# A two-layer graph network on one core: fp32 products in the first layer's sums, shorter lags at the layers' ends, and part of a normalisation on VectorE

## The chip, the core and the metric

The kernel runs on one core of a Trainium2 chip. The metric is the device time of one execution in microseconds, taken as the median of several runs. Beside it there is one profiled execution, whose trace gives the start and the length of every instruction on every engine. The engines are PE (TensorE, the matrix multiplier; its weight loads are listed as PEld), DVE (VectorE), ACT (ScalarE), POOL (GpSimd) and SP (SyncE, which here only issues DMAs). Each works through its own queue in order, and they meet through semaphores. DMAs are issued from the SP, ACT and POOL queues.

## The reference

There are 12,500 nodes with 64 features and 212,500 edges, sorted by their target `dst`. Each edge has a source `src`, a type from 0 to 15 and 8 attributes. Two layers run one after the other, and the second reads all of what the first has made:

```python
h = jnp.maximum(_layernorm(x, axis=-1), 0.0)
x = x + L0(h, weight, src, dst, edge_type)        # 16 matrices of 64 x 64
h = jnp.maximum(_layernorm(x, axis=-1), 0.0)
x = x + L1(h, src, dst, edge_attr, W1, b1, W2, b2)

# L0: sum over edges of  h[src] @ weight[type]           into dst
# L1: sum over edges of  relu([h[src], h[dst], attr] @ W1 + b1) @ W2 + b2   into dst
```

Everything is fp32.

## The kernel before

**Tiles and groups.** The edges are cut into 1,664 tiles of 128 (1,661 with edges in them), four tiles make a group (`G = 4`), and there are 416 groups (`NGR`). The nodes stand in 98 blocks of 128 (`NB`). Because the edges are sorted by target, the targets of one tile lie in a window of 12 nodes (`WT`) and those of one group in a window of 40 (`W`). A check in front finds out whether that holds; if it does, the kernel goes through `in_order()` (L272), which is what the profile shows, and otherwise through another path that the change leaves as it is.

**Front.** `x` is loaded in nine chunks of 6, 14, 14, 14, 14, 14, 12, 6 and 4 blocks (`FRONT`). For each chunk, `rows_of_sources` (L205) takes mean and variance on VectorE, the root on ScalarE, and then one ScalarE instruction per block makes `h` (L211). The SP queue writes each chunk of `h` to `h_rows` in HBM (L212).

**Gather.** `gather` (L397) issues one indirect DMA per tile from POOL (L402): 128 rows of 64 fp32 numbers, named by a column of `src_i`, into a tile `rows` that is buffered 14 deep. Both layers use it, the first with `h_rows`, the second with `a_rows`.

**First layer** (`first_layer`, L550). A loop over turns, `it`, handles several groups in one turn, each at another stage. In turn `it`, POOL gathers group `it` and ScalarE makes its one-hots, `oh_r`, over 16 relations times 12 nodes (`relations`, L410). One turn later (`L1_HI`) ScalarE rounds the gathered rows to bf16, two turns later (`L1_LO`) VectorE makes two more bf16 parts from what is left (three instructions), three turns later (`L1_PE`) PE multiplies the three parts by the bf16 one-hots, in two halves of 96 columns each, so 24 matmuls per group; and six turns later (`L1_ADD`) VectorE adds each tile's product into a table of relations by nodes (`table`), at a place that is read into a register. When the last group that touches two blocks has been added (the groups in `FIN`, at the end 408, 412 and 415), `finish` (L471) begins for these blocks: it multiplies the table by the 16 matrices (`pT`, fp32), adds to `x`, normalises, transposes, multiplies by the first two parts of `W1` and writes `a_rows` (fp32) and `b_rows` (bf16 parts) from the SP queue. `finish` is a generator; the loop takes one to three of its steps after each addition. Other generators cut in the same way are `attributes`, which splits the edge attributes into three bf16 parts, and `codes`, which makes the next piece of the one-hots' codes.

**Order.** `InOrder` (L443, whose line L452 stands for nearly all instructions of both layers in the profile) ties each engine's instructions to the order in which the program issues them. An instruction that waits therefore holds up all that was written behind it on its engine. POOL's gathers are not tied to the other engines except by their data: a gather needs a free `rows` buffer, and the first gather of a layer needs the whole of the table that it reads from, so the first layer's waits for the last write of `h_rows` and the second's for the last write of `a_rows`.

**Second layer** (`second_layer`, L653). The same kind of loop. In turn `it` POOL gathers rows of `a_rows`, SP loads `bw` and `at`, ScalarE makes one-hots and PE forms `pz`; three turns later VectorE adds the rows (`z`), four turns later ScalarE applies the relu (`hid`), six turns later PE sums over the edges by fp32 one-hots (`pa`), nine turns later VectorE adds into `sums`. `results` (L632) multiplies finished blocks by `W2`, adds `x` and writes the output from the ACT queue.

Of the kernel before, what the change touches and what calls it, by code (L numbers as in the profile page):

```python
# [37 lines left out]
ALU = mybir.AluOpType  # L39
# [37 lines left out]
L1_HI, L1_LO, L1_PE, L1_ADD = 1, 2, 3, 6  # L77
L2_Z, L2_HID, L2_PE, L2_ADD = 3, 4, 6, 9
# [38 lines left out]
def gnn_kernel(  # L117
# [69 lines left out]
    with ExitStack() as c1:  # L187
# [17 lines left out]
        def rows_of_sources(b0, nb):  # L205
            mv, rs = stats(wk, b0, nb, "r")
            off = wk.tile([P, nb], F32, name="r_off")
            V.scalar_tensor_tensor(off, mv[:, :, 0], -1.0, rs, op0=ALU.mult, op1=ALU.mult)
            h = wk.tile([P, nb, D], F32, name="r_h", bufs=4)
            for k in range(nb):  # L210
                S.activation(h[:, k, :], x3[:, b0 + k, :], AF.Relu, bias=off[:, k : k + 1], scale=rs[:, k : k + 1])  # L211
            nc.sync.dma_start(h_rows[b0 * P : (b0 + nb) * P, :].rearrange("(b p) c -> p b c", p=P), h)  # L212
# [59 lines left out]
    def in_order():  # L272
        with ExitStack() as c2:
# [36 lines left out]
            NHID = L2_PE - L2_HID + 3  # L310
# [99 lines left out]
            def relations(code, k, n):  # L410

                off = wk.tile([P, G, RW], BF16, name="off_r")
                oh = wk.tile([P, G, RW], BF16, name="oh_r", bufs=L1_PE + 2)
                for i in range(n):
                    S_.activation(off[:, i, :], iota_s, AF.Abs, bias=code[:, k + i : k + i + 1])
                S_.activation(oh[:, :n, :], off[:, :n, :], AF.Relu, bias=1.0, scale=-1.0)
                return oh

            def windows(row, k, top, engine):
                with behind(engine.engine):  # L420
                    _, vals = nc.values_load_multi_w_load_instructions(
                        row[0:1, k : k + RG],
                        engines=(engine.engine.engine,),
                        min_val=0,
                        max_val=top,
                        skip_runtime_bounds_check_because="targets are nodes, within the step's table by the check in front",
                    )
                return vals
# [33 lines left out]
            def go_on(k):  # L462

                n = BLOCKS[k][1] * P
                S_.copy(tables[(k + 1) % 2][:, :, :AHEAD], tables[k % 2][:, :, n : n + AHEAD])
# [84 lines left out]
            def first_layer(psA):  # L550
# [5 lines left out]
                n_of, oh_of, rows_of, parts_of, pa_of = {}, {}, {}, {}, {}  # L556
                chunk = 0
                for it in range(NGR + L1_ADD):
# [15 lines left out]
                    g = it - L1_HI  # L574
                    n = n_of.get(g, 0)
                    if n:
                        parts_of[g] = wk.tile([P, G, 3, D], BF16, name="parts", bufs=L1_PE + 2)
                        S_.copy(parts_of[g][:, :n, 0, :], rows_of[g][:, :n, :])
                    g = it - L1_LO
                    n = n_of.get(g, 0)  # L580
                    if n:
                        parts, left = parts_of[g], rows_of.pop(g)[:, :n, :]
                        lo = wk.tile([P, G, D], F32, name="left")[:, :n, :]
                        V_.tensor_tensor(lo, left, parts[:, :n, 0, :], op=ALU.subtract)
                        V_.tensor_copy(parts[:, :n, 1, :], lo)
                        V_.tensor_tensor(parts[:, :n, 2, :], lo, parts[:, :n, 1, :], op=ALU.subtract)
                    g = it - L1_PE
                    a = it - L1_ADD
                    if n_of.get(g, 0):

                        pa_of[g] = psA.tile([P, G, HW], F32, name="pa", bufs=5)
                    for i in range(G):
                        if i < n_of.get(g, 0):
                            for j in range(3):
                                for half in range(2):
                                    T_.matmul(
                                        pa_of[g][half * D : (half + 1) * D, i, :],
                                        lhsT=parts_of[g][:, i, j, :],
                                        rhs=oh_of[g][:, i, half * HW : (half + 1) * HW],
                                        start=(j == 0),  # L600
                                        stop=(j == 2),
                                    )
                        if a < 0:
                            continue
                        k = a * G + i
                        if i < n_of[a]:
                            ca, ka = divmod(k, NT // NCH)
                            if k % RG == 0:
                                at = windows(codes_of[ca][1], ka, SN + AHEAD - WT, V_)
                            to = tables[STEP[a] % 2][:, :, bass.ds(at[k % RG], WT)]  # L610
                            V_.tensor_tensor(
                                to, to, pa_of[a][:, i, :].rearrange("p (r n) -> p r n", r=RH), op=ALU.add
                            )
                        for _ in range(1 if a <= FIN[NREG - 1] else 2 if a <= FIN[NFIN - 2] else 3):
                            next(open_step, None)
                        next(coming, None)
                        if i % 2:
                            next(beside, None)
                    if a in FIN:
                        k = FIN.index(a)  # L620
                        for _ in open_step:
                            pass
                        if k + 1 < NFIN:
                            go_on(k)
                        open_step = finish(k, psA)
# [27 lines left out]
            def second_layer(ps):  # L653
# [6 lines left out]
                for it in range(NGR + L2_ADD):  # L660
# [39 lines left out]
                    g = it - L2_Z  # L700
                    n = n_of.get(g, 0)
                    if n:
                        z = wk.tile([P, G, D], F32, name="z", bufs=L2_HID - L2_Z + 2)
                        V_.tensor_tensor(z[:, :n, :], pz_of.pop(g)[:, :n, :], a_of.pop(g)[:, :n, :], op=ALU.add)
                        hid_of[g] = z
                    g = it - L2_HID
                    n = n_of.get(g, 0)
                    if n:
                        z = hid_of[g]
                        hid_of[g] = hid[g % NHID]  # L710
                        S_.activation(hid_of[g][:, :n, :D], z[:, :n, :], AF.Relu)
                        oh_of[g] = wk.tile([P, G, W], F32, name="oh", bufs=L2_PE - L2_HID + 2)
                        V_.tensor_tensor(
                            oh_of[g][:, :n, :],
                            bc(local[:, g * G : g * G + n], 2, W, [P, n, W]),
                            bc(iota_p, 1, n, [P, n, W]),
                            op=ALU.is_equal,
                        )
                    g = it - L2_PE
                    n = n_of.get(g, 0)  # L720
                    if n:
                        if g % 4 == 0:
                            pa = ps.tile([DA, 4, W], F32, name="pa", bufs=2)
                        pa_of[g] = pa[:, g % 4, :]
                        r, o = hid_of.pop(g), oh_of.pop(g)
                        for i in range(n):
                            T_.matmul(pa_of[g], lhsT=r[:, i, :], rhs=o[:, i, :], start=(i == 0), stop=(i == n - 1))
                    next(open_step, None)
                    g = it - L2_ADD
                    if g < 0:  # L730
                        continue
                    if n_of[g]:
                        if g % RG == 0:
                            at.update(enumerate(windows(place_row, g, SN + AHEAD2 - W, V_), g))
                        to = sums[STEP[g] % 2][:, bass.ds(at.pop(g), W)]
                        V_.tensor_tensor(to, to, pa_of.pop(g), op=ALU.add)
                    if g in FIN:
                        k = FIN.index(g)
                        for _ in open_step:
                            pass  # L740
                        if k + 1 < NFIN:
                            n = BLOCKS[k][1] * P
                            V_.tensor_copy(sums[(k + 1) % 2][:, :AHEAD2], sums[k % 2][:, n : n + AHEAD2])
                        open_step = results(k, ps)
# [459 lines left out]
```

## Time and profile before

| | |
|---|---|
| median of 3 runs | 4277.16 us (4273.73 to 4277.83) |
| profiled execution, its own time | 4275.86 us |
| its span, first to last instruction | 4274.1 us |
| busy: POOL | 3179.0 us (74%), 3,342 instructions |
| busy: ACT | 2041.7 us (48%), 4,300 instructions |
| busy: PE / weight loads | 1769.3 us (41%) / 1449.1 us (34%) |
| busy: DVE | 1421.0 us (33%), 5,311 instructions |
| HBM traffic | 56 GB/s over the span |
| granted TensorE clock | 1.00 of full speed |

A group row of the profile gives line, engine, operation, tiles and count, then busy time in all and mean ns of one, then the idle time of that engine just before these instructions and what ended it. A row of the timeline gives start and length in us, engine, line, operation, tiles, and in brackets the idle time before it and what ended that. A short line such as `DVE parts L452` in a wait names the engine, the tile and the line of what was waited for, by the profile's reckoning. A program's fp32 matmul stands in the trace as two records.

### The profile page before, as it was taken

Reading aid. Unit: us, or ns where it says so; the run is one execution under the profiler, and the core shown is the slowest. Engines: PE = TensorE matmul, PEld = TensorE weight load, DVE = VectorE, ACT = ScalarE, POOL = GpSimd, SP = SyncE. Lnnn points to the kernel's source line nnn. Section 1 sums busy time; section 2 is a strip of 40 time slices with the busy share of each in tenths; the row PEclk is TensorE's granted clock in tenths of the full one; section 3 lists DMA queues with packets and bytes.
Section 4 is the critical chain, followed back from the end, with each engine's and each line's share of the span. In section 5 each row is a group of like instructions: output and inputs, shape, how many; then the busy total and the mean of one; then the engine's idle time right before and its main releaser. Section 6 shows DMA issues by size and latency. Waiting matters only on the chain.

```text
span 4274.1 us, 61048 instructions
## 1 busy us (share of the span) xinstructions
PE 1769.3 (41%) x18622; PEld 1449.1 (34%) x18622; DVE 1421.0 (33%) x5311; ACT 2041.7 (48%) x4300; POOL 3179.0 (74%) x3342
## 2 busy tenths in 40 slices
PE   1454545555554545454543333333333333333333
PEld 1343434343343434343432222232322222232222
DVE  5444545445454454444421111111111111111111
ACT  6566666666666666565633333333333333333332
POOL 4777777777777777777757777777777777777776
DMA  5121212122222121111123333333333333333332
GB/s 128 38 43 40 47 39 47 40 44 42 44 42 43 40 42 35 30 31 30 31 67 72 71 70 73 70 69 74 70 69 74 70 69 74 69 70 74 70 72 41
DMA packets 289907, 241.93 MB, mean 57 GB/s; under 512 B 177128, under 2 KB 220144, under 8 KB 289464
## 3 DMA queue, kind: packets, MB, share of 16 engines
q0 software_dynamic: 106816, 110.79, 14.7%
q1 hardware_dynamic: 167241, 123.53, 10.7%
q10 hardware_dynamic: 15510, 3.61, 0.4%
q8 instruction: 149, 2.44, 0.2%
q14 instruction: 191, 1.56, 0.1%
HBM read 212.57 MB, written 25.10 MB: 56 GB/s over the span
## 4 chain that ended last, share of the span: by engine, by line
POOL 36%; DMA 34%; issue 19%; DVE 4%; ACT 4%; PE 1%; DVEq 0%; POOLq 0%; SPq 0%; ACTq 0%
POOL rows L402 36%; DMA rows<-h_rows,src_i 19%; DMA rows<-a_rows,src_i 14%; DVE parts L452 1%; DVE table L452 1%; DVE left L452 1%; DMA first_row<-in_first 1%; ACT parts L452 1%; ACT table L452 1%; ACT off_r L452 1%; PE pT L452 1%; PE pa L452 0%; ACT bp L452 0%; ACT attr_p L452 0%; POOLq L402 0%
## 5 line engine op out<-in xcount | busy, mean ns | idle before, releaser
L402 POOL DMA_INDIRECT rows<-h_rows,src_i x1661 | 1605.3, 966 | 545.6 <-issue 379.4
L402 POOL DMA_INDIRECT rows<-a_rows,src_i x1661 | 1567.2, 944 | 534.3 <-issue 461.8
L452 PE MATMUL pa<-oh_r,parts 128*64 128x96 bf16 x9966 | 649.3, 282 | 741.1 <-ACT parts L452 426.1
L452 ACT ACTIVATE hid<-z 128x256 f32<-128x256 f32 x416 | 173.1, 416 | 1343.4 <-DVE z L452 1309.4
L452 PE MATMUL pz<-bw,ohT 120*128 120x64 bf16 x1661 | 230.7, 240 | 1290.3 <-ACT ohT L452 1280.2
L452 PEld LDWEIGHTS <-parts 128*64 128x64 bf16 x9966 | 443.2, 158 | 927.4 <-ACT parts L452 465.7
L452 DVE TENSOR_TENSOR z<-pz,rows 128x256 f32<-128x256 f32 x416 | 176.5, 424 | 1712.7 <-DMA rows<-a_rows,src_i 1556.5
L452 PEld LDWEIGHTS <-ohT 120*128 120x128 bf16 x1661 | 165.0, 124 | 1351.5 <-ACT ohT L452 1345.1
L452 ACT ACTIVATE off_r<-iota_s,code 128x192 bf16<-128x192 f32 x1661 | 617.6, 443 | 1.7 <-DMA w1c<-w1c_p 1.7
L452 ACT CAST parts<-rows 128x256 bf16<-128x256 f32 x416 | 167.6, 403 | 736.3 <-DMA rows<-h_rows,src_i 735.8
L452 PE MATMUL pT<-wrel,table 128*128 128x64 f32 x1568 | 434.0, 434 | 113.8 <-DVE table L452 113.8
L452 DVE TENSOR_TENSOR table<-table,pa 128x96 f32 x1661 | 419.9, 253 | 123.4 <-issue 51.4
L452 PE MATMUL pa<-oh,hid 128*65 128x40 f32 x3322 | 448.4, 309 | 10.2 <-DVE sums L452 8.1
L452 PEld LDWEIGHTS pT<-wrel,table 128*128 128x128 f32 x1568 | 363.0, 323 | 161.5 <-DVE table L452 117.7
L452 PEld LDWEIGHTS pa<-oh,hid 128*65 128x65 f32 x3322 | 408.2, 230 | 10.5 <-issue 8.3
L452 DVE TENSOR_TENSOR left<-rows,parts 128x256 f32<-128x256 f32 x416 | 176.5, 424 | 565.3 <-ACT parts L452 564.1
L452 ACT ACTIVATE oh_r<-off_r 128x768 bf16<-128x768 bf16 x416 | 349.9, 841 | 13.0
L452 ACT ACTIVATE off<-local_bc,neg_w 120x512 bf16<-120x512 bf16 x416 | 294.2, 707 | 32.0 <-DVE sums L452 17.3
L452 ACT ACTIVATE ohT<-off 120x512 bf16<-120x512 bf16 x416 | 261.6, 629 | 13.0
L452 PE MATMUL pz<-w1c,at 72*128 72x64 bf16 x1661 | 232.6, 241 | 5.9 <-DMA at<-attr_p 3.9
L452 DVE TENSOR_TENSOR parts<-left,parts 128x256 bf16<-128x256 f32 x416 | 180.3, 433 | 14.2
L452 PEld LDWEIGHTS <-at 72*128 72x128 bf16 x1661 | 180.4, 128 | 7.1 <-DMA at<-attr_p 7.1
(103 smaller groups left out, 1096.1 us busy)
## 6 DMA issues: line engine op xcount, KB each, us to landing
local_bc<-dst_l SPq DMA_DIRECT2D x104, 480.0 KB
at<-attr_p SPq DMA_DIRECT2D x416, 72.0 KB
rows<-h_rows,src_i POOLq DMA_INDIRECT x1661
rows<-a_rows,src_i POOLq DMA_INDIRECT x1661
attr_p<-attr_p SPq DMA_DIRECT2D x78, 128.0 KB
attr_a<-in_attr_t SPq DMA_DIRECT2D x26, 256.0 KB
bw<-b_rows SPq DMA_DIRECT2D x416, 15.0 KB
b_rows<-bp SPq DMA_DIRECT2D x48, 96.0 KB
```

The lines of the kernel that those rows point to most:

```text
L402: G_.indirect_dma_start(out=t[:, i, :], out_offset=None, in_=table, in_offset=bass.IndirectOffsetOnAxis(ap=idx[:, k : k + 1], axis=0),)
L452: last_ins[self.engine] = getattr(self.engine, name)(*args, **kw)
```

## The change

**Products.** The first layer no longer cuts the gathered rows into bf16 parts. PE takes the gathered fp32 rows as weights and fp32 one-hots as the moving operand: two matmuls per tile, one for each half, instead of six. ScalarE's cast and VectorE's three instructions per group go, and with them the tiles `parts` and `left`. `oh_r` becomes fp32, four buffers instead of five.

**Lags.** Each lag becomes a pair (most, least), and `turns` lists which groups come up in which turn: up to group 379 a group comes up `most` turns after its gather, and from there the lag falls by one every four groups down to `least`. The first layer's products come two turns after the gather, at the end one; its additions five, at the end two. In the second layer the lags 3, 4, 6 and 9 all fall to one. A turn can hold more than one group of a stage, so the stages became loops over lists. The register values of the places are kept in a dictionary. `hid` has six buffers instead of five and `oh` five instead of four.

**Front.** In chunks of seven blocks or more, ScalarE makes `h` for the first six sevenths of the blocks (12 of 14, 10 of 12), and VectorE makes the others with two instructions per chunk.

```diff
-L1_HI, L1_LO, L1_PE, L1_ADD = 1, 2, 3, 6
-L2_Z, L2_HID, L2_PE, L2_ADD = 3, 4, 6, 9
+L1_PE, L1_ADD = (2, 1), (5, 2)
+L2_Z, L2_HID, L2_PE, L2_ADD = (3, 1), (4, 1), (6, 1), (9, 1)
+def turns(lag):
+    most, least = lag
+    of = {}
+    for g in range(NGR):
+        of.setdefault(g + max(least, min(most, most - (g - (NGR - 40)) // 4)), []).append(g)
+    return of
...
-            for k in range(nb):
+            on_s = nb * 6 // 7 if nb >= LB // 2 else nb
+            for k in range(on_s):
                 S.activation(h[:, k, :], x3[:, b0 + k, :], AF.Relu, bias=off[:, k : k + 1], scale=rs[:, k : k + 1])
+            if on_s < nb:
+                v = slice(on_s, nb)
+                shape = [P, nb - on_s, D]
+                V.tensor_tensor(h[:, v, :], x3[:, b0 + on_s : b0 + nb, :], bc(mv[:, v, 0], 2, D, shape), op=ALU.subtract)
+                V.scalar_tensor_tensor(h[:, v, :], h[:, v, :], 0.0, bc(rs[:, v], 2, D, shape), op0=ALU.max, op1=ALU.mult)
...
-                oh = wk.tile([P, G, RW], BF16, name="oh_r", bufs=L1_PE + 2)
+                oh = wk.tile([P, G, RW], F32, name="oh_r", bufs=L1_PE[0] + 2)
...
-                        S_.copy(parts_of[g][:, :n, 0, :], rows_of[g][:, :n, :])
...
-                        V_.tensor_tensor(lo, left, parts[:, :n, 0, :], op=ALU.subtract)
-                        V_.tensor_copy(parts[:, :n, 1, :], lo)
-                        V_.tensor_tensor(parts[:, :n, 2, :], lo, parts[:, :n, 1, :], op=ALU.subtract)
...
+                def products(g, i):
+                    for half in range(2):
+                        T_.matmul(
+                            pa_of[g][half * D : (half + 1) * D, i, :],
+                            lhsT=rows_of[g][:, i, :],
+                            rhs=oh_of[g][:, i, half * HW : (half + 1) * HW],
+                            start=True,
+                            stop=True,
+                        )
...
+                    now, adds = of_pe.get(it, []), of_add.get(it, [])
...
+                    for j in range(max(len(now), len(adds))):
+                        for i in range(G):
+                            if j < len(now) and i < n_of[now[j]]:
+                                products(now[j], i)
+                            if j >= len(adds):
+                                continue
+                            a = adds[j]
+                            add(a, i)
+                            for _ in range(1 if a <= FIN[NREG - 1] else 2 if a <= FIN[NFIN - 2] else 3):
+                                next(open_step, None)
...
+                        if j < len(adds) and adds[j] in FIN:
...
+                            open_step = finish(k, psA)
...
-                for it in range(NGR + L2_ADD):
+                of_z, of_hid, of_pe, of_add = turns(L2_Z), turns(L2_HID), turns(L2_PE), turns(L2_ADD)
+                for it in range(NGR + L2_ADD[1]):
```

`add(a, i)` holds the addition of tile `i` of group `a` into the table, as it stood in the loop before.

## The prediction

> **What bounds the kernel now.** I read the chain that ended last first, then the two gather groups, then the timeline at a stalled gather and at the four ends: front, first layer, change of layer, tail.
>
> ```profile
> POOL 36%; DMA 34%; issue 19%; DVE 4%; ACT 4%; PE 1%; DVEq 0%; POOLq 0%; SPq 0%; ACTq 0%
> ...
> L402 POOL DMA_INDIRECT rows<-h_rows,src_i x1661 | 1605.3, 966 | 545.6 <-issue 379.4
> L402 POOL DMA_INDIRECT rows<-a_rows,src_i x1661 | 1567.2, 944 | 534.3 <-issue 461.8
> ```
>
> The chain runs through POOL's indirect DMAs: each layer issues 1,661 of them, 128 rows each, on one in-order queue, while PE, ACT and DVE are idle half the time or more. In the timeline the second layer's gathers start 1.248 us apart on average (0.944 busy, 0.305 between) and the first layer's 1.271. The span is therefore 49.72 us of front, 2111.2 us of first gathers, 28.36 us in which POOL waits, 2073.1 us of second gathers and 11.7 us of tail. Work of PE, ACT and DVE inside a layer costs nothing unless it slows POOL.
>
> Something does slow POOL in the first layer alone. Two of its gathers, with VectorE's rows beside them (start, duration):
>
> ```profile
> 2143.29 0.42 DVE L452 TENSOR_TENSOR left<-rows,parts 128x256 f32<-128x256 f32 x1
> 2143.46 1.07 POOL L402 DMA_INDIRECT rows<-h_rows,src_i  x1 [0.30 <-issue]
> ...
> 2148.44 0.43 DVE L452 TENSOR_TENSOR parts<-left,parts 128x256 bf16<-128x256 f32 x1
> 2148.58 1.11 POOL L402 DMA_INDIRECT rows<-h_rows,src_i  x1 [0.30 <-issue]
> ```
>
> Each gather begins while a VectorE instruction with two SBUF inputs runs, and is longer by the time for which that instruction runs on after the gather's start, less 0.13 us: 0.25 in the first pair, which costs 0.13, and 0.29 in the second, which costs 0.17. I laid all 1,661 gathers over VectorE's rows this way. Together they take 38.1 us beyond 0.944 each, and the instruction that ends 0.127 us plus that excess after the gather's start is `parts<-left,parts` for 17.5 us (86 gathers), the cast `parts<-left` for 3.1, `left<-rows,parts` for 2.6; the attribute splits (`attr_r`, `attr_p`) for 9.2, the codes, `local_o` and single cases for the rest. The second layer's total excess is 0.5 us.
>
> The wait between the layers, the front's end and the tail:
>
> ```profile
> 38.52 6.07 ACT L211 ACTIVATE r_h<-x_sb,r_off,r_rs 128x64 f32<-128x64 f32 x18 [0.31 <-DVE r_off L208]
> 45.22 1.43 ACT L211 ACTIVATE r_h<-x_sb,r_off,r_rs 128x64 f32<-128x64 f32 x4 [0.44 <-DVE r_off L208]
> 49.72 1.01 POOL L402 DMA_INDIRECT rows<-h_rows,src_i  x1 [39.75 <-DMA seq<-in_dst]
> ...
> 2159.97 0.94 POOL L402 DMA_INDIRECT rows<-h_rows,src_i  x1 [0.30 <-issue]
> 2163.28 0.24 ACT L452 CAST parts<-rows 128x64 bf16<-128x64 f32 x1 [1.57 <-DMA rows<-h_rows,src_i]
> 2170.91 3.65 PE L452 MATMUL pT<-wrel,table 128*128 128x64 f32 x16 [2.26 <-DVE table L452]
> 2179.65 3.65 PE L452 MATMUL pT<-wrel,table 128*128 128x64 f32 x16 [1.89 <-DVE table L452]
> 2186.83 0.32 SPq L452 DMA_DIRECT2D a_rows<-ab  x1
> 2189.28 0.94 POOL L402 DMA_INDIRECT rows<-a_rows,src_i  x1 [28.36 <-issue]
> ...
> 4264.79 0.22 DVE L452 TENSOR_TENSOR z<-pz,rows 128x64 f32<-128x64 f32 x1 [0.45 <-DMA rows<-a_rows,src_i]
> 4269.81 0.22 DVE L452 TENSOR_TENSOR o<-po,x_sb 128x64 f32<-128x64 f32 x1 [0.84 <-PE po L452]
> ```
>
> The first gather waits for the last `h_rows` write, behind ACT's 98 normalisations. The second layer's first waits for the last `a_rows` write: two single-block finishes (`pT`) run one behind the other after the last rows have landed.
>
> **The change part by part.**
>
> *Products in fp32.* Removed per group: ACT's cast (0.40 us), VectorE's three (0.42, 0.30, 0.43), 24 bf16 matmuls. All of it lies under POOL's 4.99 us per group (4 x 1.248), so its own time is worth nothing; what counts is the excess that the three VectorE instructions cause, 17.5 + 3.1 + 2.6 = **23.2 us**. The additions into the table read PSUM and one SBUF operand, and no excess ends with them, so what stays on VectorE does not take it over. The Trainium skill (SBUF — State Buffer, Who interferes with whom) says that an instruction with two SBUF inputs holds the shared read port for its whole length, that GpSimd's SBUF read waits for it, and that whoever came first has it. Taken alone, with gathers falling at random, that would be (0.425² + 0.30² + 0.434²) / (2 x 1.248) = 0.184 us per group, 76 us in 415 groups. The trace has 23.2 because the instructions follow the rows' landing and so keep a phase to POOL; I take 23.2. Ends: 14, if the attribute and code instructions meet gathers 9 us more often in their new places, and 30, if half of the 14.9 us that others cause goes too.
>
> What it adds is PE work. Four tiles x two halves x two recorded passes (the rows of fp32 `pT` and `pa<-oh,hid` show two per matmul) are 16 passes per group of 64 weight columns and 96 moving. No row has this form. Passes follow each other by 213 ns where 128 columns are loaded (`pT`) and 110 where 65 are (`pa<-oh,hid`): 1.67 ns per loaded column, 107 for 64, 1.7 us per group. The skill speaks against the change here: FP8 and Floating Point Precision, TensorE Precision Notes, gives true fp32 four passes. The bf16 halves of 96 columns start 40 ns apart on average (pairs 79), so four are 160 per half, 1.3 us per group against 0.96 for three bf16 products. Above, `pab<-w1ab,hT` (64 x 128, 128 moving) has pairs of passes 373 ns apart, 187 each: 3.0 us. I take 2.0, near the first row, whose column count is closest. PE's other work in this layer, start to start, is 397 + 34 + 19 us, 1.09 per group, so PE has 3.1 (at most 4.1) of 4.99: hidden, at 0 us. The cover ends at 3.9 us of products, 244 ns a pass. `oh_r` in fp32 costs ACT no more: fp32 copies run at 0.92 ns per element (1.89 us for 2048), the bf16 row at 0.84 us for 768 is no faster in slope, and ACT's 1.49 + 0.84 per group is far under 4.99.
>
> *Shorter lags at the first layer's end.* The addition of group 415 moves from turn 421 to 417, of 412 from 418 to 414, of 408 from 414 to 410. The finish of block 96 then runs while POOL still gathers: its 16 `pT` passes come between the products of group 414 at about 2158 to 2161 and its normalisation ends at 2162.5. On PE the product of group 415 stands ahead of that finish's transpose and waits for rows that land at 2163.3 (2.36 after the gather ends). Then: product 0.7 us to 2164.0, transpose to `bp` 3.3 us (2176.20 to 2179.37 now), addition at 2167.4, and the last finish as now from `pT` to the gather, 2189.28 - 2179.65 = 9.6: 2177.1. The wait becomes 16.2 instead of 28.36: **12.1 us**. Ends 9 (finish 96 wholly behind the landing) and 15 (nothing left of it, 13.3 us of wait).
>
> *Shorter lags at the second layer's end.* In front of it `z`, `hid`, product and addition follow within a turn, about 2 us against a group's 4.99. After the last landing: `z` at 4264.79, `hid` to 4265.36, two passes 0.45, addition 0.2, `po` 0.75, so `o` at 4266.8 instead of 4269.81: **3.0 us**, ends 2 and 3.5. The deeper `hid` and `oh` buffers cost nothing.
>
> *VectorE's share in front.* Blocks of 14 give 2, the block of 12 gives 2: 12 normalisations less on ACT at 0.331 us (14 in 4.73, less the last one's latency), 4.0 us. VectorE adds 12 instructions of about 0.29 us, 3.5 us in all, beside 5.7 us of idle time in front of its last reciprocals; but near 17 us ACT waits for its statistics, which come 0.5 us later, so the second chunk's saving is lost: **3.0 us**, ends 1.5 and 4. POOL issues nothing there, so the two-input instructions stall nobody. The wait moves to the last chunks, which stay on ACT; the SP queue's `h_rows` writes wait for both engines.
>
> Sum: 3.0 + 23.2 + 12.1 + 3.0 = 41.3. The profiled execution took 4275.86 us (span 4274.1, 1.8 around it), giving 4234.6; the median of the runs, 4277.16, lies 1.3 above, giving **4236**.
>
> **The rivals.** *PE becomes the bound (slower).* The last fp32 transpose with 128 moving columns holds off the next bf16 pass by 405 ns; scaled to 96 that is 304 a pass, 4.86 us per group, 5.95 with the rest, 0.96 over POOL, about 400 us in 415 groups. It decides from 244 ns: at 255, (16 x 0.255 + 1.09 - 4.99) x 415 = 75, less 41: 4310. Against it, 350 follows `pT` too, whose passes stand 213 apart, so a good part is the switch of type. 0.06.
> *The stalls stay.* The remaining two-input instructions lock onto the gathers' starts as `parts` did, and the layer gains 5 or less: 4236 + 18 = 4254. For it: 35 of the 52 attribute instructions stall a gather even now. 0.12.
> *The lags do nothing*, because finish 96 still stands wholly behind the last rows: 12.1 goes to 2, 4246. 0.08.
> *No change on balance*, a loss of some 40 us elsewhere: nothing in the profile names it. 0.02.
> The likeliest has 0.72.
>
> **How the numbers follow.** Ends of the parts: 1.5 + 14 + 9 + 2 = 26.5 and 4 + 30 + 15 + 3.5 = 52.5, so 4224 to 4251; the first two rivals below 41 reach 4254, where the range ends. PE's case lies outside. 0.2%, 8.6 us, is about what a measurement of this kernel can tell from no change. Faster 0.92, same 0.03, slower 0.05.
>
> **What would show it.** First-layer gathers at a mean of 0.945 to 0.955 us (now 966 ns in the row) and no excess above 0.2 us but at attributes and codes; POOL's longest wait 14 to 19 us; first gather near 46.7; span's end 8.7 us after the last gather. Products with passes above 0.24 us, POOL waiting on PE for `rows`, would prove it wrong.

## The result and the profile after

The changed kernel takes 4237.61 us (median of 4 runs, 4236.6 to 4238.22), the kernel before 4277.49 beside it (4273.73 to 4280.76): ratio 0.9907, 95% interval 0.989 to 0.9924, so 0.9% faster. 4236 was predicted. The profiled execution took 4236.6 us with a span of 4234.8; 4234.6 was worked out for it. The five stretches of the span, cut at the gathers:

| stretch (us) | before | after | gained | predicted |
|---|---|---|---|---|
| front, to the first gather | 49.72 | 45.27 | 4.45 | 3.0 |
| first layer, first gather to the end of its last | 2111.20 | 2090.60 | 20.6 | 23.2 |
| wait between the layers | 28.36 | 16.36 | 12.0 | 12.1 |
| second layer | 2073.11 | 2073.10 | 0.0 | 0 |
| tail | 11.69 | 9.43 | 2.26 | 3.0 |
| sum | 4274.1 | 4234.8 | 39.3 | 41.3 |

The page of the profile after: the chain that ended last, then three groups of instructions (times | busy us, mean ns | idle before, what ended most of it).

```profile
POOL 44%; DMA 29%; issue 23%; PE 5%; ACT 0%; POOLq 0%; DVE 0%; DVEq 0%; ACTq 0%
...
L419 POOL DMA_INDIRECT rows<-h_rows,src_i x1661 | 1584.7, 954 | 542.1 <-issue 418.8
L419 POOL DMA_INDIRECT rows<-a_rows,src_i x1661 | 1567.2, 944 | 522.3 <-issue 457.7
L469 PE MATMUL pa<-oh_r,rows 128*64 128x96 f32 x6644 | 932.1, 391 | 747.3 <-DMA rows<-h_rows,src_i 656.1
```

The chain still runs through POOL's gathers. The first layer's have a mean of 954 ns instead of 966, the second layer's are where they were: what the gathers take beyond 0.944 us each sank from 38.6 us (38.1 by the prediction's count) to 18.1. The new fp32 products idle until rows have landed (656 us of their 747), so PE waits for POOL and not POOL for PE.

The timeline after, in order of time: the front's end, two gathers that still stall, the change of layer, the tail.

```profile
34.74 5.41 ACT L223 ACTIVATE r_h<-x_sb,r_off,r_rs 128x64 f32<-128x64 f32 x16 [0.31 <-DVE r_off L218]
40.77 1.43 ACT L223 ACTIVATE r_h<-x_sb,r_off,r_rs 128x64 f32<-128x64 f32 x4 [0.44 <-DVE r_off L218]
45.27 1.01 POOL L419 DMA_INDIRECT rows<-h_rows,src_i  x1 [36.16 <-DMA seq<-in_dst]
...
744.39 0.69 DVE L469 TENSOR_TENSOR attr_r<-attr_a,attr_p 128x512 f32<-128x512 f32 x1 [2.84 <-ACT attr_p L469]
744.47 1.44 POOL L419 DMA_INDIRECT rows<-h_rows,src_i  x1 [0.30 <-issue]
...
1611.48 0.29 DVE L469 TENSOR_TENSOR bp<-ab,bp 128x128 bf16<-128x128 f32 x1 [0.20 <-ACT bp L469]
1611.53 1.06 POOL L419 DMA_INDIRECT rows<-h_rows,src_i  x1 [0.30 <-issue]
...
2134.93 0.94 POOL L419 DMA_INDIRECT rows<-h_rows,src_i  x1 [0.30 <-issue]
2142.32 0.25 DVE L469 TENSOR_TENSOR table<-table,pa 128x96 f32 x1
2142.72 3.65 PE L469 MATMUL pT<-wrel,table 128*128 128x64 f32 x16 [1.89 <-DVE table L469]
2149.78 0.32 SPq L469 DMA_DIRECT2D a_rows<-ab  x1
2152.24 0.94 POOL L419 DMA_INDIRECT rows<-a_rows,src_i  x1 [16.36 <-issue]
...
4228.18 0.21 DVE L469 TENSOR_TENSOR z<-pz,rows 128x64 f32<-128x64 f32 x1
4230.25 0.23 DVE L469 TENSOR_TENSOR o<-po,x_sb 128x64 f32<-128x64 f32 x1 [0.78 <-PE po L469]
```

Three things are to be seen. The split's two-input instructions are gone, but an attribute instruction (`attr_r`) still lengthens a gather by 0.49 us, and a short instruction of the finish (`bp`), which did so once before, now costs 0.12. Between the layers stands one `pT` block instead of two. In the tail `o` begins 2.07 us after the last `z`, where it was 5.02.

### The profile page after: what moved, and what is told of

Read it like the earlier page. It is cut to its first block, busy times and chain, and to the rows that moved or that the text cites. A ratio compares the mean times of both kernels' runs of the same rounds, so it can differ in the third digit from the quotient of the medians.

```text
span 4234.8 us, 51468 instructions
## 1 busy us (share of the span) xinstructions
PE 2048.8 (48%) x15300; PEld 1509.6 (36%) x15300; DVE 971.8 (23%) x4076; ACT 1884.2 (44%) x3872; POOL 3158.4 (75%) x3342
## 4 chain that ended last, share of the span: by engine, by line
POOL 44%; DMA 29%; issue 23%; PE 5%; ACT 0%; POOLq 0%; DVE 0%; DVEq 0%; ACTq 0%
POOL rows L419 43%; DMA rows<-h_rows,src_i 15%; DMA rows<-a_rows,src_i 13%; PE pT L469 3%; PE pa L469 2%; DMA first_row<-in_first 1%; POOLq L419 0%; PE pab L469 0%; ACT table L469 0%; DVE sums L469 0%; DVE z L469 0%; ACT hid L469 0%; DMA a_rows<-ab 0%; ACT off_r L469 0%; POOLq L1210 0%
## 5 line engine op out<-in xcount | busy, mean ns | idle before, releaser
L419 POOL DMA_INDIRECT rows<-h_rows,src_i x1661 | 1584.7, 954 | 542.1 <-issue 418.8
L419 POOL DMA_INDIRECT rows<-a_rows,src_i x1661 | 1567.2, 944 | 522.3 <-issue 457.7
L469 PE MATMUL pa<-oh_r,rows 128*64 128x96 f32 x6644 | 932.1, 391 | 747.3 <-DMA rows<-h_rows,src_i 656.1
L469 PEld LDWEIGHTS pa<-oh_r,rows 128*64 128x64 f32 x6644 | 502.3, 208 | 1107.4 <-DMA rows<-h_rows,src_i 759.5
L469 ACT ACTIVATE oh_r<-off_r 128x768 f32<-128x768 bf16 x416 | 350.0, 841 | 183.8 <-PE pa L469 173.0
L469 ACT COPY table<-zero_c 128x2048 f32<-128x2048 f32 x49 | 93.0, 1897 | 476.0 <-PE pT L469 461.6
L469 DVE TENSOR_TENSOR oh<-local,iota_p 128x160 f32<-128x160 f32 x416 | 128.8, 310 | 0.0
L469 DVE TENSOR_TENSOR x_sb<-x_sb,pT 128x128 f32<-128x128 f32 (+1 forms) x50 | 14.3, 285 | 430.5 <-PE pT L469 430.5
```

The lines of the kernel that those rows point to most:

```text
L419: G_.indirect_dma_start(out=t[:, i, :], out_offset=None, in_=table, in_offset=bass.IndirectOffsetOnAxis(ap=idx[:, k : k + 1], axis=0),)
L469: last_ins[self.engine] = getattr(self.engine, name)(*args, **kw)
```

## The experiments

The first layer's gathers were compared in each run by the time they take beyond 0.944 us each (below: the excess), and that time was put down to the VectorE instruction that ends as the gather gets going, as in the prediction.

**VectorE's share in front, alone.** The kernel before with this one edit:

```diff
-            for k in range(nb):
+            on_s = nb * 6 // 7 if nb >= LB // 2 else nb
+            for k in range(on_s):
...
+            if on_s < nb:
...
+                V.tensor_tensor(h[:, v, :], x3[:, b0 + on_s : b0 + nb, :], bc(mv[:, v, 0], 2, D, shape), op=ALU.subtract)
+                V.scalar_tensor_tensor(h[:, v, :], h[:, v, :], 0.0, bc(rs[:, v], 2, D, shape), op0=ALU.max, op1=ALU.mult)
```

> The kernel before with VectorE's share of h in front and nothing else. My theory: the first gather starts 3 us earlier (1.5 to 4.5), near 46 instead of 49.7, and all later stretches keep their lengths (2111 of first gathers, 28.4 of waiting, 2073 of second gathers, 11.7 of tail): about 4274 us. Rival, that the earlier front in the changed kernel came from x landing earlier in that one execution: the first gather stays near 49 and the time near 4277.

4271.91 us (4270.2 to 4275.03), ratio 0.9991 (0.9982 to 1.0); in the profiled executions the first gather starts at 45.83 us instead of 49.72, and the other four stretches are within 0.1 us of before. The share is worth 3.9 us in the profile and touches nothing else. In the whole time it is at the edge of what the measurement can tell from nothing.

**The products and the shorter constant lags, alone.** The changed kernel with the share off and lags that don't shrink:

```diff
-L1_PE, L1_ADD = (2, 1), (5, 2)
-L2_Z, L2_HID, L2_PE, L2_ADD = (3, 1), (4, 1), (6, 1), (9, 1)
+L1_PE, L1_ADD = (2, 2), (5, 5)
+L2_Z, L2_HID, L2_PE, L2_ADD = (3, 3), (4, 4), (6, 6), (9, 9)
...
-            on_s = nb * 6 // 7 if nb >= LB // 2 else nb
+            on_s = nb
```

> The changed kernel with constant lags (2 and 5 in the first layer; 3, 4, 6 and 9 in the second) and all of h in front on ScalarE: the fp32 products alone. Port theory: the first gathers take 20 to 23 us less than 2111, mean of one near 954 ns; the front stays at 49 to 50, the wait between the layers at 25 to 28.4 (the drain is one turn shorter), the tail at 11.7: 4250 to 4256 us. Rival, that the shorter lags also helped inside the layer: the first gathers come out 5 us or more longer than in the changed kernel.

4251.2 us, ratio 0.9942 (0.9926 to 0.9959). Its first layer is 2088.86 us long: the loop's gain is all here. The wait between the layers is 24.62, and the tail 12.33. The timeline of this run at the change of layer:

```profile
2138.29 0.95 POOL L419 DMA_INDIRECT rows<-h_rows,src_i  x1 [0.30 <-PE pa L469]
...
2145.51 3.65 PE L469 MATMUL pT<-wrel,table 128*128 128x64 f32 x16 [2.25 <-DVE table L469]
...
2154.24 3.65 PE L469 MATMUL pT<-wrel,table 128*128 128x64 f32 x16 [1.89 <-DVE table L469]
...
2163.86 0.94 POOL L419 DMA_INDIRECT rows<-a_rows,src_i  x1 [24.62 <-issue]
```

The two finishes still run one behind the other, 8.73 us apart. But the first begins 6.3 us after the last gather's end, not 10.0 as before, since no cast and no split stand in front of the product. So of the 12.0 us, 3.7 belong to the products and their one turn less of lag, and 8.3 to the shrinking lags, which also bring 2.9 of the tail (12.33 to 9.43).

**Is it the second SBUF input that slows POOL?** Two runs put three VectorE instructions per group back into the changed kernel, as large as those removed and read by nobody. One gives them SBUF operands, the other one PSUM operand each; in both, `pa` has four buffers instead of five.

```diff
+                k0 = own.tile([P, G, D], BF16, name="k0")
...
+                        V_.tensor_tensor(left[:, :n, :], rows_of[g][:, :n, :], k0[:, :n, :], op=ALU.subtract)
+                        V_.tensor_copy(k1[:, :n, :], left[:, :n, :])
+                        V_.tensor_tensor(k2[:, :n, :], left[:, :n, :], k1[:, :n, :], op=ALU.subtract)
```

> The changed kernel with three VectorE instructions per group put back, on the gathered rows and on constants, with results that nobody reads: two subtractions with two SBUF inputs and a cast from SBUF, in the same forms and two turns after the gather (pa has four buffers instead of five). Port theory: gathers are held again, by 10 to 40 us in all over the 18 of the changed kernel, the mean of one near 960 to 978 ns, 4248 to 4278 us. Rival, that the gain came from less work on PE and ACT or from free rows buffers: 4236 to 4241.

The second of the pair:

```diff
+                kp = psA.tile([P, G, D], F32, name="kp", bufs=1)
...
+                        V_.tensor_tensor(left[:, :n, :], rows_of[g][:, :n, :], kp[:, :n, :], op=ALU.subtract)
+                        V_.tensor_copy(k1[:, :n, :], kp[:, :n, :])
+                        V_.tensor_tensor(k2[:, :n, :], left[:, :n, :], kp[:, :n, :], op=ALU.subtract)
```

> As e3_two_sbuf, but each of the three VectorE instructions takes one of its inputs, the cast its only one, from PSUM: same count, nearly the same length, at most one SBUF input each (pa has four buffers). Port theory: no gather is held by them, mean of one 953 to 956 ns, 4236 to 4241 us. Rival, that VectorE's load as such slows the gathers: as e3_two_sbuf, 4248 or more.

With SBUF operands 4268.69 us, ratio 0.9981 (0.9975 to 0.9988): 31 of the 40 us gained are gone, and the first layer takes 2120.5 us, longer than in the kernel before. With PSUM operands 4234.35, ratio 0.9901 (0.9884 to 0.9917), a little under the 4236 that was expected at the least. The groups in the page of the first:

```profile
L419 POOL DMA_INDIRECT rows<-h_rows,src_i x1661 | 1614.6, 972 | 542.2 <-issue 356.6
...
L469 DVE TENSOR_TENSOR left<-rows,k 128x256 f32<-128x256 f32 x416 | 180.8, 435 | 871.9 <-DMA rows<-h_rows,src_i 871.8
...
L469 DVE TENSOR_TENSOR k<-left,k 128x256 bf16<-128x256 f32 x416 | 177.0, 425 | 14.2
```

And in that of the second:

```profile
L419 POOL DMA_INDIRECT rows<-h_rows,src_i x1661 | 1581.2, 952 | 542.6 <-issue 347.7
...
L469 DVE TENSOR_TENSOR left<-rows,kp 128x256 f32<-128x256 f32 x416 | 174.8, 420 | 959.7 <-DMA rows<-h_rows,src_i 959.6
...
L469 DVE CAST k<-kp 128x256 bf16<-128x256 f32 x416 | 173.2, 416 | 0.0
```

The instructions are nearly equally long and wait for the same rows, yet the gathers take 972 ns in one run and 952 in the other. The excess is 47.9 us with SBUF operands: 20.1 ends with `k<-left,k` (138 gathers), 13.9 with `left<-rows,k` (73), 0.3 with the cast. With PSUM operands it is 14.7, and none of it ends with an added instruction, though VectorE is busy for 1388.7 us there against 971.8 in the changed kernel. So VectorE's load costs nothing here.

Nor is it that the second run's instructions miss the gathers' starts. With SBUF operands 136 gathers start while `left<-rows,k` has 0.15 us or more to go, with PSUM operands 119 while `left<-rows,kp` has. Of the 136, 70 are lengthened, by up to 0.26 us; of the 119 none by more than 0.01. First two gathers with SBUF operands, then one with PSUM operands:

```profile
110.87 0.50 DVE L469 TENSOR_TENSOR left<-rows,k 128x256 f32<-128x256 f32 x1 [2.54 <-DMA rows<-h_rows,src_i]
110.92 0.94 POOL L419 DMA_INDIRECT rows<-h_rows,src_i  x1 [0.30 <-issue]
...
121.00 0.43 DVE L469 TENSOR_TENSOR left<-rows,k 128x256 f32<-128x256 f32 x1 [2.54 <-DMA rows<-h_rows,src_i]
121.05 1.19 POOL L419 DMA_INDIRECT rows<-h_rows,src_i  x1 [0.30 <-issue]
```

```profile
79.41 0.42 DVE L469 TENSOR_TENSOR left<-rows,kp 128x256 f32<-128x256 f32 x1 [2.70 <-DMA rows<-h_rows,src_i]
79.46 0.94 POOL L419 DMA_INDIRECT rows<-h_rows,src_i  x1 [0.30 <-issue]
```

In the first two the gather starts 0.05 us after the subtraction, a few nanoseconds less in one than in the other. A gather that starts up to 0.044 us after the subtraction is not lengthened; there the subtraction is, to as much as 0.50 us instead of 0.43. From 0.046 us on it is the gather. One of the two waits, and it is the one that came second.

So what costs is the second SBUF input of an instruction that is under way when a gather starts. This is what the Trainium skill (SBUF — State Buffer, Who interferes with whom) says of two SBUF inputs. But two inputs are not the whole of it, since a cast has only one. In the kernel before, 55 gathers start while the cast `parts<-left` has 0.15 us or more to go. The 17 that start within 0.041 us of it keep their length; the 38 that start 0.046 us or more after it are all lengthened, by 0.04 to 0.12 us, 3.1 us in all:

```profile
82.67 0.29 DVE L452 CAST parts<-left 128x256 bf16<-128x256 f32 x1
82.77 1.01 POOL L402 DMA_INDIRECT rows<-h_rows,src_i  x1 [0.30 <-issue]
```

Of 34 gathers that start under the cast from PSUM (`k<-kp`) none is lengthened. Not every instruction with one SBUF input stalls, though: none of 16 does that start under the statistics (`s_st<-x_sb`) in the run with SBUF operands. The split had cost 23.2 us in the kernel before and costs 34.3 here, with the same three forms of instruction in other places: how much of it meets a gather is a matter of phase.

**How much room has PE?** The products were issued twice and three times over, each time into the same place. First the double:

```diff
-                    for half in range(2):
+                    for half in (0, 1) * 2:
```

> The changed kernel with each product issued twice (the second overwrites the first), so PE has 32 passes per group. From the trace of the changed kernel a pair of halves takes 215 ns, so a group's products go from 1.7 to 3.4 us, with 1.09 of other work 4.5 of POOL's 4.99. Theory that PE is hidden: first gathers within 5 us of 2090.6, the wait between the layers up to 2 us longer, 4236 to 4242 us. Rival, that PE's pass is nearer to 0.2 us in the long run or that PE's order leaves no slack: 6.2 or more per group, 4700 us and up.

Then the triple, `(0, 1) * 3`:

> The changed kernel with each product issued three times: 5.2 us of products and 1.09 of other PE work per group, 6.3 against POOL's 4.99. Theory: PE becomes the bound, POOL waits for rows buffers, the first layer takes (6.25 - 5.03) x 415 = 500 us more, 4740 us, between 4650 and 4800. If PE's other work overlaps the loads of the products: 5.2 per group, 70 us more, 4310.

Twice: 4236.1 us, ratio 0.9896 (0.9879 to 0.9912), no different from once. Three times: 4229.87 in one execution, where 4740 had been expected. That expectation was wrong. It was built on the 215 ns by which a tile's second pair of halves follows its first in the changed kernel, 1.7 us of products per group. The page of the triple, its granted clock in the 40 slices and its gathers, shows where:

```profile
PE   2777778877777777777743333333333333333333
...
PEclk9987987798898988998855555555555555555555
...
L419 POOL DMA_INDIRECT rows<-h_rows,src_i x1661 | 1576.9, 949 | 542.0 <-issue 404.4
```

The double's row of the clock:

```profile
PEclk9565555555555555555655555555555555555555
```

One triple product in the timeline of the triple:

```profile
1000.21 3.88 PE L469 MATMUL pa<-oh_r,rows 128*64 128x96 f32 x48
```

The 48 passes of a whole tripled group take 3.88 us, 81 ns each; the last twelve of them fall into a stretch of full clock. In the trace the two halves of a tile mostly start 6 to 9 ns apart. Where the record of the clock says 0.5, most of these pairs follow each other by 160 ns, and the first after a pause by 215; where it says 1.0, they come every 83 ns. So a group's products, done in one go, are 8 x 160 ns = 1.3 us at the lower clock, and by this estimate the triple fits under POOL's 4.99 even there (3 x 1.28 + 1.09 = 4.93). On top of that the clock rises with PE's work: it is 0.55 over the double's span, and 0.84 to 0.88 in stretches of the triple's first layer. The faster first layer of the triple (excess 10.4 us) is not a gain of the products: the attribute instructions stall the gathers for 5.3 us instead of 9.6, and `bp` and `s_h` for 0.2 instead of 3.3. Everything behind the products has moved, which would explain it; that was not tested by itself.

**Where does PE begin to bind?** Eight times, `(0, 1) * 8`:

> The changed kernel with each product issued eight times: 64 pairs of passes per group. Theory after e6_products_thrice, that a busy PE gets the full clock and a pair then takes about 80 ns: 5.1 us of products and 0.6 to 1.1 of other work per group, 5.7 to 6.2 against POOL's 4.99, so PE becomes the bound, POOL waits for rows buffers and the first layer takes 280 to 490 us more: 4520 to 4730 us. If the pair stayed at 155 ns: 11 us per group, about 6700 us.

This ran on a chip where the kernel before takes 5549.54 us. 6953.61 us in one execution, against the 4520 to 4730 expected, which was worked out for a chip like the others. The 6700 that pairs of 155 ns would give is near, but not for that reason: the clock is 0.84 to 0.87 in the first layer, and most of the pairs come every 83 ns. POOL's waits in this run (us in total, times, longest):

```profile
POOL rows L419 <- PE pa L469: 2239.8, 402, 12.7
```

The same row of the changed kernel:

```profile
POOL rows L419 <- PE pa L469: 4.6, 15, 0.3
```

Nearly every one of 415 groups now holds POOL until PE is done: PE as the bound does show itself in this row. How long the cover is can't be read from here. A group takes 10.1 us, while its 128 passes at the 41 to 49 ns of this run's long stretches of passes would be 5.3 to 6.2; the remainder is time in which PE waited for nothing that the profile shows. So the point at which products bind on one of the other chips was not measured, except that it lies beyond three.

**The largest stall that is left.** The attribute instructions' rest is put into PSUM, which takes a copy more on ACT; `pa` has four buffers.

```diff
-                rest = wk.tile([P, ACH], F32, name="attr_r")
+                rest = psA.tile([P, ACH], F32, name="attr_r", bufs=1)
...
+                S_.copy(rest, a)
...
-                V_.tensor_tensor(rest, a, parts[:, 0, :], op=ALU.subtract)
+                V_.tensor_tensor(rest, rest, parts[:, 0, :], op=ALU.subtract)
```

> The changed kernel with the rest of the split attributes held in PSUM (one more ScalarE copy per chunk, pa with four buffers), so the 52 attribute subtractions have one SBUF input each. Port theory: the 9.6 us of excess that end with them go, first gathers near 2081 us, mean of one near 948 ns, 4227 to 4231 us. Rival, that any VectorE instruction of 0.69 us holds the gathers: 4237.

4228.24 us (4227.77 to 4228.69), ratio 0.9879 (0.9862 to 0.9895): faster than both kernels. The gathers in its page:

```profile
L420 POOL DMA_INDIRECT rows<-h_rows,src_i x1661 | 1575.6, 949 | 542.0 <-issue 409.9
```

And a gather in its timeline that starts while `attr_r` has 0.44 us to go:

```profile
1099.34 0.70 DVE L470 TENSOR_TENSOR attr_r<-attr_r,attr_p 128x512 f32<-128x512 f32 x1 [3.20 <-ACT attr_p L470]
1099.60 0.94 POOL L420 DMA_INDIRECT rows<-h_rows,src_i  x1 [0.30 <-issue]
```

Eighteen gathers start while an attribute instruction has 0.15 us or more to go, and none is lengthened. Of the excess, 9.0 us stay, and none ends with an attribute instruction. The first layer is 9.2 us shorter (2081.44), close to what these instructions had cost (9.6), for 26 ACT copies of 0.58 us, which lie on an engine that POOL doesn't wait for.

**A larger share in front.** Four of each 14 blocks on VectorE instead of two:

```diff
-            on_s = nb * 6 // 7 if nb >= LB // 2 else nb
+            on_s = nb * 5 // 7 if nb >= LB // 2 else nb
```

> The changed kernel with VectorE's share of h in front doubled (4 of 14, 4 of 12 blocks). If ScalarE still sets the front's end: another 11 to 12 activations of 0.331 less, the first gather 2 to 4 us earlier, near 43, 4234 to 4236 us. If the landing of x or VectorE's own statistics set it by then: 0 to 1 us, 4237.

4234.07 us (4232.29 to 4235.39), ratio 0.9892 (0.9876 to 0.9909); the first gather starts at 44.37. Twelve more normalisations taken from ACT would be 4.0 us; what is left of that is 0.9 against the changed kernel, 1.7 against the mean of the runs with the smaller share. The time lies in the range of the first case, but 1.9 of its 3.5 us below the changed kernel come from the first layer (2088.70), which this edit doesn't touch. ACT in this run's timeline:

```profile
29.15 3.42 ACT L223 ACTIVATE r_h<-x_sb,r_off,r_rs 128x64 f32<-128x64 f32 x10 [1.23 <-DVE r_off L218]
33.65 0.30 ACT L183 ACTIVATE r_rs<-r_mv,eps 128x12 f32<-128x12 f32 x1 [1.09 <-DVE r_mv L182]
```

ACT now waits 1.23 and 1.09 us for VectorE's statistics: the two engines are near balance in front, and little more is to be had there.

**Both of these together.** The two diffs above in one kernel:

> e7_attr_psum and e8_front_5of7 in one kernel. If the two gains add up: first gather near 44.4, first gathers near 2081, 4225 to 4228 us, some 10 us below the changed kernel. If the earlier start of the gathers brings stalls back: 4228 or more.

It ran on the chip of the eightfold product, and its time there, 5148.82 us against 5549.54 (ratio 0.9275, 0.9262 to 0.9288), says nothing about 4225 on the others. The same kernel once more:

> The same kernel as e9_attr_and_front (the attribute's rest in PSUM, and 4 of 14 blocks in front on VectorE), on a chip where the kernel before takes its usual 4277. If the two edits are independent: front end near 44.4 as in e8, loop of the first layer near 2081.5 as in e7, together 4224 to 4228, excess of the first layer's gathers over 944 ns near 9 us. If the long waits of e9_attr_and_front come from the kernel and not from that chip: a gap between the layers near 60 and a time above 4900.

This was yet another chip, with 5476.28 us for the kernel before and 5099.54 for this one (ratio 0.9318, 0.9306 to 0.9331). The gap between the layers is 59.96 us in one and 59.97 in the other, as the expectation said for a cause in the kernel; but the kernel before is 1,200 us longer there too, so the chip is at least part of it, and without a profile of the kernel before on such a chip the two can't be told apart. The stalls did behave as in the run of the attributes alone: a mean of 946 ns. The product in the page of the second of these runs:

```profile
L470 PE MATMUL pa<-oh_r,rows 128*64 128x96 f32 x6644 | 845.3, 371 | 962.9 <-issue 748.9
```

Here PE idles 748.9 us in front of its products for nothing that the profile shows, where the changed kernel's PE waits for rows. The gathers themselves take no more time on these chips (0.946 and 0.943 us in the mean in this run); the time lies between them, in POOL's idle time (866.6 and 1039.0 us before the two groups, 542.1 and 522.3 in the changed kernel). The cause is open. The change takes PE from 24 recorded products a group to 16; whether that is why it gains 7% on these chips and 0.9% on the others was not tested. Whether the two edits add up on the other chips stays open as well; the fastest version measured there is the one with the attribute rest in PSUM alone.

## Why the prediction was right, point by point

**The loop** (23.2 said, 20.6 measured). The mechanism is shown by the pair of runs with and without a PSUM operand; only that the cast stalls too, which the sum counted, does not follow from two SBUF inputs. The three rows that the sum was made of went to nothing, all 23.2 us. The term that was mis-sized is the assumption that nothing takes their place: with other work gone, the finish's `bp<-ab,bp` (1.7 us in 30 gathers) and `s_h<-x_sb,s_mv` (1.6 in 22) now lie across gathers' starts, where each had cost 0.1 before. The range's lower end had reckoned with such a shift, but put it on the attributes and codes; the attributes rose only from 9.2 to 9.6. That the predicted signs held, a mean of 954 ns and, but for two gathers at `local_o`, no single excess above 0.2 us outside attributes and codes, doesn't make the small ones nothing. The reason for 23.2 instead of 76, a phase kept to POOL, was not needed either. The 76 leaves out the 0.127 us that the prediction's own rule takes off, and that a gather within about 0.045 us of the instruction's start isn't lengthened. With both, the same sum is (0.253² + 0.128² + 0.262²) / (2 x 1.248) = 0.060 us per group, 25 us in 415 groups, an estimate for gathers that fall at random.

**PE's cover** (3.1 of 4.99 us said). The conclusion held: products cost no time. The price of 2.0 us was too high. Passes of 64 loaded and 96 moving columns come every 80 ns on average at the lower clock when they follow without a pause, hence 1.3 us per group. That is the value that four passes gave (FP8 and Floating Point Precision, TensorE Precision Notes, in the Trainium skill: an fp32 product is four passes). The row of `pT`, with 107 ns for 64 columns, which I preferred because its column count was nearest, is what the changed kernel shows as long as its products come tile by tile (215 a pair), but not what they take when PE has more to do. The rival in which PE binds was further off than its price of 244 ns a pass said, since three times the products did not bind.

**The wait between the layers** (16.2 said, 16.36 measured). The sums came as worked out: last addition 6.4 us after the last gather's end (said 6.5), then 9.9 us from there to the next gather (said 9.7). The steps inside the 6.4 did not quite. The finish of block 96 was to be normalised 1.6 us after the last gather's end, before the last product; its last four `pT` passes came after that end, and it was normalised at 3.3. So its transpose waited for the normalisation and not for the product, 0.3 us later than said, and the way from there to `bp` was 0.2 shorter. That these cancel is luck. The prediction gave all 12.1 us to the shrinking lags; the run without them shows that 3.7 come from the products.

**The tail** (3.0 said, 2.26 measured). From the last `z` to `o` 2.0 us were said, and 2.07 measured. But `z` now begins 2.85 us after the last gather's end instead of 2.40, because the group before it has moved up and its own addition, at 4228.07, stands in front on VectorE: 0.45 lost. From the start of `o` to the end it took 4.51 us instead of 4.27, for which the runs give no reason. Moving work up to the end also moved a neighbour in front of it, and that step was missing in the prediction.

**The front** (3.0 said, 4.45 measured; 3.9 alone). I let 1.0 us go because the saving of the second chunk, the first of 14 blocks, would be lost to a wait for statistics. It isn't: from that chunk's start on ACT to the next one's are 5.77 us before and 4.86 after. From its first normalisation to the end of the last of all took 34.24 us before and 30.80 after, 3.44 less. The other 1.01 us is its earlier start (11.40 instead of 12.41); with the share alone it is 11.98, and I can't say what of it the change does. Over the seven profiled runs with the same share, on chips where the kernel before takes its usual time, the first gather starts at 46.07 on average, in the two without it at 50.05: 4.0 us.

The errors of the parts, +1.45, -2.6, -0.1 and -0.74, cancel in part, which is why 4236 came so near, and that is luck; the 2.0 us that remain are about the spread between runs of one kernel (1.6 here).

## What to carry to other kernels

When an in-order queue on POOL sets the time, look at which of VectorE's instructions are under way as POOL's start: those with two SBUF inputs lengthened them here, and so did some casts from SBUF. One operand in PSUM was enough to stop it, with VectorE busier than before. Count this by phase, from the trace, and expect the instructions that stay to drift into new phases: here that took a tenth of the gain. Shortening a pipeline's lags at its end was worth the work that stood in series behind the last landing, less what moves up beside it.

## What the hardware showed that was not expected

**A granted clock of 1.00 can be an empty record.** The profiles of the kernel before and after say 1.00 throughout, and their records hold no clock event at all. Yet `pT`'s passes mostly stand 215 ns apart there, and never closer than 210. The record of the triple has events, and its `pT` passes stand 210 or more apart in all 237 cases where it says 0.5, and 110 to 160 in all 947 where it says 1.0. One run (with PSUM operands) has an event in the middle, where its row falls from 9s to 5s:

```profile
PEclk9999999655555555555555555555555555555555
```

`pT`'s passes are 215 ns apart on both sides of it. So PE ran at half speed in both kernels, and the spacing of passes tells more than the recorded clock. The Trainium skill (TensorE: Matmul & The Clock Gate, Part 1: The HAM clock gate) gives an idle array half the clock and a busy one the full; the triple agrees with it, at 0.84 to 0.88 where the double has 0.58 to 0.59. So PE's cover grew as PE was given more to do.

**Instructions that nobody changed moved the time by up to 7 us,** as they met the gathers at another phase: the attribute instructions cost 9.6 us in the changed kernel and 5.3 in the triple, `bp` and `s_h` 3.3 and 0.2.
